# Graph tile periods: output biases and part of a table's weighing moved from VectorE to GpSimd

## The chip, the cores and the metric

The kernel runs on one core of a Trainium2 chip. The metric is the device time of one execution in microseconds. The core has TensorE (PE: matrix products), VectorE (DVE), ScalarE (ACT) and GpSimd (POOL) as computing engines, each with its own queue that is worked off in order; SyncE (SP) and GpSimd issue the transfers that are spoken of here. Times of the timeline count from the start of the profiled span.

## The reference

Two layers work on 625 nodes with 1024 features and 10,000 edges. What matters here is the first layer, which adds a graph attention and a linear attention to x, and then a small quantised feed-forward block:

```python
xn = _layernorm(x, axis=-1)
x = x + _L0_gnn_ref(xn, edge_index, ...) + _L0_mix_ref(xn[None], ...)[0]
x = x + _L0_ffn_ref(_layernorm(x, axis=-1)[None], ...)[0]
xn = _layernorm(x, axis=-1)
...
# in _L0_gnn_ref: softmax over the edges of a node, per head, then the weighted sum of rows
p = jnp.exp(e - m[dst])
denom = jax.ops.segment_sum(p, dst, num_segments=n)
alpha = p / (denom[dst] + 1e-16)
out = jax.ops.segment_sum(alpha[..., None] * xl[src], dst, num_segments=n)
out = out.reshape(n, HID)
return out @ W_up
# the end of _L0_mix_ref
return out @ W_o + b_o
```

`b_o` is the output bias, a row of 1024 that is added to every node.

## The kernel before, in words

The 625 nodes are cut into NT = 5 tiles of P = 125. The scores of all edges (4 heads) have been scattered into a table in HBM, indexed by source and destination. `CT` in SBUF holds how often each pair of nodes is an edge. The attention of tile t is then a dense product: the table's columns of tile t are weighed with `CT`, which gives `pT` (5 source tiles of 125 x 4 x 125), and `pT` is multiplied with the rows `xl1`.

The part of the code that is changed runs in periods p = 0 to 6, one tile entering per period. The functions, with their lines in the kernel before:

- `load_table(t)` (L851) loads the table's part for tile t into a tile `tb`, in two transfers issued by GpSimd.
- `weigh(t)` (L858) makes `pT`: five multiplications, one for each source tile s (L865), of `tb` (read with a step of four words, since the heads lie innermost) by `CT`, 125 x 500 each, all on VectorE. A second path of the program, `shifted`, is for other data and is not the one that runs here.
- `sums(t)` (L888) multiplies on TensorE: for each head, over s = 0 to 4 in this order, into the PSUM tile `pg`; then VectorE divides by the sums (`dens`, `den`, `go`, L898 to L902).
- `turn_sums(t)` transposes `go` (`pgoT`), and ScalarE copies it (`goT`). `up_again(t)` (L920) multiplies by `W_up` into `px`, which already holds the linear attention's output product, and VectorE adds `px` to x (L933).
- `add_bias(t, ...)` (L1070, L1074) adds the output bias to x, in two halves of 512 columns per tile. For t = 3 it adds `kept`, which holds the linear attention's output with its bias.
- `ffn(t)` (L964) is the feed-forward block of tile t, in steps `p1` (layer norm statistics, L950 to L975, and quantisation, L958 to L962, into `room`), `f1` (transposes, L985), `f2` (product `pgu` and gating), `f3` (transposes, `hT`, L1017), `f4` (product `pdn`, added to x, L1033), `p5` (layer norm for the next layer, L1040) and `f5` (transposes, L1048).
- `mixed(4, ...)` (L764) and `spacer()` (key and value products of the next layer, `pk` and `pv`, with `bk_t` and `bv_t` as biases) put other matrix products between these.

What is issued first runs first on each engine; TensorE's work is handed out through a small stream object, `do`, which issues each product one step before what follows it. Before the first period, GpSimd issues the loads of table 0, of x tile 0, of table 1, and of x tiles 1 to 4, each tile in two transfers; after them in its queue come the memset of `xnT1` (L1093), the load of `bq` (L238), and the loads of tables 2, 3 and 4 as buffers come free. The tiles `tb`, `pT`, `kept` and others share a pool of four buffers (`mid`).

Before the loop stand `load_table(0)`, the loads of x with `load_table(1)` between them, and `weigh(0)`. In period p come, in this order: the last steps of the feed-forward of tile p - 2, the first of tile p - 1, `sums(p)`, `turn_sums(p)`, `weigh(p + 1)`, `load_table(p + 2)`, the biases of this period, further feed-forward steps and `up_again(p)`. The biases of tiles 0 and 1 are added at the end of period 0, of tile 3 at the end of period 1, and of tiles 2 and 4 near the start of period 2.

Of the kernel before, what the change touches and what calls it, by code (L numbers as in the profile page):

```python
# [14 lines left out]
ALU = mybir.AluOpType  # L15
# [6 lines left out]
P = 125  # L22
# [20 lines left out]
def gps_kernel(tc: tile.TileContext, w: dict, out: bass.AP):  # L43

    again = attempt(tc, w, out, False)
    with tc.If(again > 0):
        attempt(tc, w, out, True)  # L50
# [3 lines left out]
def attempt(ctx: ExitStack, tc: tile.TileContext, w: dict, out: bass.AP, shifted: bool):  # L54

    nc = tc.nc
# [101 lines left out]
    def nodes(t):  # L158
        return slice(t * P, (t + 1) * P)
# [18 lines left out]
    def rows_dma(eng, dst, src):  # L178

        return [eng.dma_start(out=dst[lo:hi], in_=src[lo:hi]) for lo, hi in ((0, 112), (112, P))]  # L180
# [5 lines left out]
    CT = CTr if shifted else CTr.bitcast(FP)  # L186
# [38 lines left out]
    def mid(shape, name):  # L225
        return midp.tile(shape, FP, tag="mid", name=name)

    def bigT(name):
        return big.tile([128, KC, NP], FP, tag="big", name=name, padded_shape=[128, KC, 640])
# [133 lines left out]
    with ExitStack() as st0:  # L363
# [8 lines left out]
        with ExitStack() as edges:  # L372
# [385 lines left out]
            def mixed(t, ks=range(KC), keep=None, then=None, paced=True, cs=(0, 1)):  # L758
                for c in cs:
                    def pe(c=c):  # L760
                        if c == 0 and ks[0] == 0:
                            hold["px", t] = ps2("px1")
                        for k in ks:
                            made = nc.tensor.matmul(hold["px", t][:P, c, :], lhsT=oT[:, k, nodes(t)], rhs=wo[c](k),  # L764
                                                    start=(k == 0), stop=(k == KC - 1 and keep is not None))
                        latest["pe"] = made.ins.name

                    def after():
                        px = hold.pop(("px", t))
                        for c in range(2):  # L770
                            nc.vector.tensor_tensor(keep[:, c, :], px[:P, c, :], bo[c][:P], op=ALU.add)

                    do(None, pe, after if keep is not None and c == 1 else None)
                    if then is not None and c == 0:
                        then()
                    if paced:
                        work(0.87 * len(ks))
# [49 lines left out]
            bo = [lin.bias(w["L0_bo"], c, tag) for c, tag in enumerate(("bk_t", "bv_t"))]  # L827
# [4 lines left out]
            kept = mid([P, 2, 512], "kept")  # L832
# [14 lines left out]
        x = xpool.tile([P, NT, D], FP, name="x")  # L847
# [3 lines left out]
        def load_table(t):  # L851

            hold["tb", t] = mid([P, NT, P, 4], "tb")
            if not shifted:
                rows_dma(nc.gpsimd, hold["tb", t].rearrange("p s d h -> p s (d h)"),
                         tview[:, :, t * 4 * P:(t + 1) * 4 * P])

        def weigh(t):  # L858

            tb, pT = hold.pop(("tb", t)), mid([P, NT, 4, P], "pT")  # L860
            hold["pT", t] = pT
            if shifted:
                exps(t, tb)
            for s in range(NT):
                nc.vector.tensor_tensor(pT[:, s], tb[:, s].rearrange("p d h -> p h d"),  # L865
                                        CT[:, s, nodes(t)].unsqueeze(1).to_broadcast([P, 4, P]), op=ALU.mult)

        def exps(t, tb):

            for h in range(4):  # L870
                sc = mix.tile([P, NP], FP, tag="qe", name="sc", bufs=1)[:, 0:N].unsqueeze(2)
                nc.sync.dma_start(out=sc, in_=table[0:N * N, :].rearrange("(t p s) h -> t p s h", t=NT, p=P)
                                  [t][:, :, h:h + 1])
                mx = late.tile([P, 1], FP, tag="mx", name="mx", bufs=1)
                nc.vector.tensor_reduce(mx, sc, AX.XY, ALU.max)
                nc.vector.tensor_scalar(mx, mx, -1.0, None, op0=ALU.mult)
                nc.scalar.activation(sc, sc, AF.Exp, bias=mx, scale=1.0)
                for s in range(NT):
                    def pe():
                        pp = ps1("pexT")  # L880
                        nc.tensor.transpose(pp[:P, :P], sc[:, nodes(s), 0], ident[:P, :P])
                        nc.vector.tensor_copy(tb[:, s, :, h], pp[:P, :P])

                    do(None, pe)
# [3 lines left out]
        def sums(t):  # L888
            pT = hold.pop(("pT", t))

            def pe():
                pg4 = hold["pg"] = ps1("pg")[:, :260].rearrange("p (h e) -> p h e", h=4)
                for h in range(4):
                    group(pg4[:P, h, :], [(pT[:, s, h, :], xl1[:, s, h, :]) for s in range(NT)])

            def after():
                pg4 = hold["pg"]
                nc.vector.tensor_scalar(dens[:, t, :], pg4[:P, :, 64], 1e-16 if shifted else 1e-30, None, op0=ALU.add)  # L898
                den = late.tile([P, 4], FP, tag="den", name="den", bufs=2)
                nc.vector.reciprocal(den, dens[:, t, :])  # L900
                go = hold["go"] = late.tile([P, 4, 64], FP, tag="go", name="go", bufs=1)
                nc.vector.tensor_tensor(go, pg4[:P, :, 0:64],  # L902
                                        den.unsqueeze(2).to_broadcast([P, 4, 64]), op=ALU.mult)

            do(None, pe, after)
# [147 lines left out]
            return p1, f1, f2, f3, f4, p5, f5  # L1053


        load_table(0)
        for t in range(NT):
            rows_dma(nc.gpsimd, x[:, t, :], xrows[t])
            if t == 0:
                load_table(1)  # L1060
        weigh(0)
        kv_pieces = iter([(f, t) for t in range(NT) for f in ("key", "value")])
        made_of = {}

        def spacer():

            f, t = next(kv_pieces)
            getattr(lin1, f)(t)

        def add_bias(*ts):  # L1070
            for t in ts:
                for c in range(2):
                    xc = x[:, t, c * 512:(c + 1) * 512]
                    nc.vector.tensor_tensor(xc, xc, kept[:, c, :] if t == 3 else bo[c][:P], op=ALU.add)  # L1074

        for p in range(NT + 2):
            do()
            if p >= 2 and p != NT:
                made_of[p - 2][5]()
            if 1 <= p <= NT:  # L1080
                made_of[p - 1] = ffn(p - 1)
                made_of[p - 1][0]()
            if p == 1:
                mixed(4, cs=(0,))
            if p == 2:
                add_bias(2, 4)
            if p >= 3:
                spacer()
            if p >= 2 and p != NT:
                made_of[p - 2][6]()  # L1090
            if p == 0:
                xnT1 = bigT("xnT1")
                nc.gpsimd.memset(xnT1[:, :, N:NP], 0.0)  # L1093
                lin1 = LinearAttention(xnT1, ("L1_Wq", "L1_Wk", "L1_bk", "L1_Wv", "L1_bv"), w["L1_bq"],
                                       lambda us: None, nc.gpsimd)
                lin1.large = True
            if p < NT:
                sums(p)
            if 1 <= p <= NT:
                made_of[p - 1][1]()  # L1100
                do()
                if p == NT:
                    made_of[p - 2][5]()
                made_of[p - 1][2]()
                if p == NT:
                    made_of[p - 2][6]()
            do()
            if p < NT:
                turn_sums(p)
            if p + 1 < NT:  # L1110
                weigh(p + 1)
            if p + 2 < NT:
                load_table(p + 2)
            if p < 2:
                add_bias(*((0, 1), (3,))[p])
            if p == 1:
                mixed(4, cs=(1,))
                lin1.weights(0)
                lin1.half(0, loaded=True)
            if 2 <= p <= NT:  # L1120
                spacer()
            if 1 <= p <= NT:
                made_of[p - 1][3]()
            do()
            if p < NT:
                up_again(p)
            if 1 <= p <= NT:
                made_of[p - 1][4]()
# [625 lines left out]
    for i in range(3):  # L1754
        d = 1 << i
# [240 lines left out]
```

## Time and profile before

| What | Value |
|---|---|
| median of 3 runs (range) | 2218.25 us (2213.3 to 2223.8) |
| profiled execution: its time, its span | 2215.67 us, 2213.9 us |
| TensorE clock granted, mean over the span | 0.979 of full speed |
| stretch 425 to 437 us: PE busy, DVE busy, POOL busy, share of the DMA engines | 0.00, 0.52, 6.83 us, 0.61 |
| stretch 437 to 454 us: PE, DVE, POOL, DMA | 13.91, 9.86, 4.55 us, 1.02 |
| stretch 454 to 489 us: PE, DVE, POOL, DMA | 28.27, 23.37, 1.40 us, 0.53 |
| stretch 489 to 506 us: PE, DVE, POOL, DMA | 15.40, 10.50, 3.27 us, 0.27 |
| stretch 506 to 590 us: PE, DVE, POOL, DMA | 77.00, 59.43, 0.00 us, 0.10 |
| L865, a weighing of 125 x 500 on VectorE, 25 of them | 1040 ns each |
| L1074, a bias addition of 125 x 512 on VectorE, 10 of them | 682 ns each |
| L1249, an addition of 125 x 1024 on GpSimd (later stage), 10 of them | 2348 ns each (median) |

A line of the timeline gives the start, the time from start to end of a group of like instructions, the engine, the line of the kernel, the operation, what it writes and reads, and how many; the bracket gives the idle time of that engine just before, and what ended it. A line of the waits gives who waited for whom, then the sum in microseconds, how often, and the longest. Busy times of neighbouring instructions overlap slightly, so a row of five weighings takes 4.84 us and not 5 x 1.04.

### The profile page before, as it was taken

To read this page: it belongs to the slowest core of one execution; us is meant where nothing else is said; L and a number is where in the kernel's file an instruction comes from. 1 tells how busy PE (TensorE), PEld (TensorE's weight loads), DVE (VectorE), ACT (ScalarE), POOL (GpSimd) and SP (SyncE) were. 2 spreads that over 40 slices of the span, in tenths; PEclk is the share of its full clock that TensorE was granted. 3 is DMA by queue.
4 is the path that set the end of the run, shared out by engine and by line. 5 is a ranking of instruction groups with operands and counts; after the bars stand their busy time and mean duration, and the time that the engine had idled before them with its cause. 6 is when DMAs were issued, how large, how long until landed. Compare 5 with 4: busy or idle time off the path is not lost. (4 is left out here: it accounts for less than half of the span.)

```text
span 2213.9 us, 17370 instructions
## 1 busy us (share of the span) xinstructions
PE 2113.7 (95%) x6934; PEld 1211.5 (55%) x6934; DVE 713.6 (32%) x1214; ACT 193.9 (9%) x354; POOL 340.0 (15%) x349
## 2 busy tenths in 40 slices
PE   8999899489899999999999999999999999999998
PEld 6565475255455777754446767457744444444443
DVE  5776378367532660000123133322011111111012
ACT  2000110012211100000000111100000000000000
POOL 1666656500000100210000000110000000000011
PEclk9999999789999999999999999999999999999999
DMA  7532263351122110240213111022099988997742
GB/s 221 201 101 82 79 199 104 74 155 33 39 86 76 48 38 1 86 149 32 76 38 105 38 38 38 28 96 89 8 362 344 330 309 294 330 330 285 277 141 91
DMA packets 145848, 301.62 MB, mean 136 GB/s; under 512 B 12370, under 2 KB 22436, under 8 KB 145754
## 3 DMA queue, kind: packets, MB, share of 16 engines
q1 hardware_dynamic: 123700, 244.23, 31.1%
q0 software_dynamic: 17376, 46.42, 7.0%
q10 hardware_dynamic: 4678, 9.72, 1.4%
q8 instruction: 58, 0.95, 0.2%
q14 instruction: 36, 0.29, 0.0%
HBM read 277.49 MB, written 22.84 MB: 136 GB/s over the span
## 5 line engine op out<-in xcount | busy, mean ns | idle before, releaser
L137 PE MATMUL pu<-w,xgT 128*128 128x512 f32 x768 | 333.9, 593 | 1.9 <-DVE xgT L1290 1.9
L137 PEld LDWEIGHTS pu<-w,xgT 128*128 128x128 f32 x768 | 144.0, 190 | 174.8 <-issue 172.0
L137 PE MATMUL pyb<-w,hb 128*128 128x512 f32 x384 | 174.3, 598 | 2.5 <-ACT yb L105 2.1
L137 PE MATMUL pq<-xnT,w 128*128 128x313 f32 x512 | 141.0, 435 | 7.0 <-DVE v L293 7.0
L137 PE MATMUL pv<-w,xnT 128*125 128x512 f32 x320 | 143.9, 600 | 3.7 <-issue 3.1
L137 PE MATMUL pk<-w,xnT 128*125 128x512 f32 x320 | 142.9, 598 | 1.8 <-issue 1.4
L137 PE MATMUL p<-tT,w 128*128 128x313 f32 x512 | 136.3, 428 | 0.4 <-DVE tT L1290 0.4
L137 PEld LDWEIGHTS pq<-xnT,w 128*128 128x128 f32 x512 | 98.9, 194 | 47.3 <-DVE v L293 7.8
L137 PEld LDWEIGHTS pyb<-w,hb 128*128 128x128 f32 x384 | 69.8, 189 | 90.9 <-issue 74.8
L1830 DVE TENSOR_TENSOR su<-pu,su 128x512 f32<-128x512 f32 x24 | 16.6, 691 | 314.6 <-ACT su L1829 314.6
L137 PEld LDWEIGHTS p<-tT,w 128*128 128x128 f32 x512 | 96.8, 190 | 37.9 <-issue 1.2
L137 PEld LDWEIGHTS pv<-w,xnT 128*125 128x125 f32 x320 | 60.2, 190 | 79.1 <-issue 77.4
L137 PEld LDWEIGHTS pk<-w,xnT 128*125 128x125 f32 x320 | 59.8, 189 | 73.9 <-issue 73.2
L641 POOL DMA_INDIRECT table<-es,at x79 | 84.6, 1071 | 61.2 <-issue 30.6
L1813 POOL DMA_INDIRECT xg<-rows_d,slots x12 | 11.3, 943 | 524.8 <-PE pxg L1820 449.0
L621 POOL DMA_INDIRECT ga<-xl_d,si x79 | 79.3, 1004 | 46.8 <-issue 21.6
L621 POOL DMA_INDIRECT gb<-xr_d,di x79 | 80.6, 1021 | 25.8 <-issue 25.8
L764 PE MATMUL px<-w,oT 128*125 128x512 f32 x160 | 69.8, 594 | 2.1 <-DVE x L933 1.4
L1179 DVE TENSOR_TENSOR z<-pz,z 125x512 fp32r<-125x512 f32 x10 | 6.9, 692 | 196.8 <-ACT z L1177 196.8
L137 PE MATMUL px<-w,hT 128*125 128x512 f32 x160 | 70.3, 592 | 0.0
L137 PE MATMUL px<-w,oT 128*125 128x512 f32 x160 | 70.3, 592 | 0.0
L137 PE MATMUL ph<-meanT,w 128*128 128x313 f32 x256 | 70.1, 426 | 0.0
(363 smaller groups left out, 2521.5 us busy)
## 6 DMA issues: line engine op xcount, KB each, us to landing
w<-in_eW_dram SPq DMA_DIRECT2D x144, 1024.0 KB
w<-in_L_Wk_dram SPq DMA_DIRECT2D x8, 1024.0 KB
w<-in_L_Wv_dram SPq DMA_DIRECT2D x8, 1024.0 KB
w<-in_L_Wq_dram SPq DMA_DIRECT2D x8, 1024.0 KB
w<-in_L_Wo_dram SPq DMA_DIRECT2D x8, 1024.0 KB
w<-in_W_self_dram SPq DMA_DIRECT2D x8, 1024.0 KB
w<-in_W_neigh_dram SPq DMA_DIRECT2D x8, 1024.0 KB
w<-in_sW_dram SPq DMA_DIRECT2D x8, 1024.0 KB
```

The source lines that it names most:

```text
L137: made = nc.tensor.matmul(dst, lhsT=lhsT, rhs=rhs, start=(i == 0), stop=(i == len(pairs) - 1))
L621: got = nc.gpsimd.indirect_dma_start(out=ab[g][side][0:p, j, :], out_offset=None, in_=src[:, :], in_offset=bass.IndirectOffsetOnAxis(ap=ix ...
L641: nc.gpsimd.indirect_dma_start(out=table[:, :], out_offset=bass.IndirectOffsetOnAxis(ap=at[0:p, lo + j:lo + j + 1], axis=0), in_=es[0:p, l ...
L764: made = nc.tensor.matmul(hold["px", t][:P, c, :], lhsT=oT[:, k, nodes(t)], rhs=wo[c](k), start=(k == 0), stop=(k == KC - 1 and keep is no ...
L1179: nc.vector.tensor_tensor(low, src, high.bitcast(FP), op=ALU.subtract)
L1813: nc.gpsimd.indirect_dma_start(out=xg, out_offset=None, in_=rows_d[:, :], in_offset=bass.IndirectOffsetOnAxis(ap=slots[:, b:b + 1], axis=0))
L1830: nc.vector.tensor_tensor(su, pu[:, 0, :], su, op=ALU.mult)
```

## The change

Three edits in the periods of the first layer:

1. `weigh`: of the five source tiles, s = 0 to 2 stay on VectorE and s = 3 and 4 are issued on GpSimd, in each of the five periods.
2. `add_bias` issues on GpSimd and no longer on VectorE.
3. Its calls move: tiles 0 and 1 before the loop, after the loads of x and ahead of `weigh(0)`; tiles 2, 4 and 3 together at the end of period 0, after `weigh(1)` and `load_table(2)`.

```diff
             for s in range(NT):
-                nc.vector.tensor_tensor(pT[:, s], tb[:, s].rearrange("p d h -> p h d"),
-                                        CT[:, s, nodes(t)].unsqueeze(1).to_broadcast([P, 4, P]), op=ALU.mult)
+                eng = nc.vector if shifted or s < 3 else nc.gpsimd
+                eng.tensor_tensor(pT[:, s], tb[:, s].rearrange("p d h -> p h d"),
+                                  CT[:, s, nodes(t)].unsqueeze(1).to_broadcast([P, 4, P]), op=ALU.mult)
...
+        def add_bias(*ts):
+            for t in ts:
+                for c in range(2):
+                    xc = x[:, t, c * 512:(c + 1) * 512]
+                    nc.gpsimd.tensor_tensor(xc, xc, kept[:, c, :] if t == 3 else bo[c][:P], op=ALU.add)
+
         load_table(0)
         for t in range(NT):
             rows_dma(nc.gpsimd, x[:, t, :], xrows[t])
             if t == 0:
                 load_table(1)
+        add_bias(0, 1)
         weigh(0)
...
-        def add_bias(*ts):
-            for t in ts:
-                for c in range(2):
-                    xc = x[:, t, c * 512:(c + 1) * 512]
-                    nc.vector.tensor_tensor(xc, xc, kept[:, c, :] if t == 3 else bo[c][:P], op=ALU.add)
...
-            if p == 2:
-                add_bias(2, 4)
...
-            if p < 2:
-                add_bias(*((0, 1), (3,))[p])
+            if p == 0:
+                add_bias(2, 4, 3)
```

GpSimd's queue thus reads, after the last load of x: four additions (tiles 0 and 1), the two weighings of table 0, the memset, the load of `bq`, the two weighings of table 1, the load of table 2, six additions (tiles 2, 4 and 3), the two weighings of table 2, the load of table 3, the loads of `bk_t` and `bv_t` for the next layer, a memset, the weighings of table 3, the load of table 4 and the weighings of table 4. The products on TensorE keep their order.

## The prediction

> **What bounds the kernel now.** I read the page first, for the limiting engine, then the waits of the stretch that the change touches (425 to 625 us), then the timeline of that stretch engine by engine, because a change in one stage is worth what the wait that ends last there is worth.
>
> ```profile
> PE 2113.7 (95%) x6934; PEld 1211.5 (55%) x6934; DVE 713.6 (32%) x1214; ACT 193.9 (9%) x354; POOL 340.0 (15%) x349
> ```
>
> TensorE is busy 95% of the span and VectorE 32%, so work taken off VectorE pays only where TensorE stands still for VectorE. The waits of this stretch say where that is:
>
> ```profile
> PE pg L137 <- DVE pT L865: 32.2, 5, 31.1
> POOL x L180 <- DMA tb<-table: 7.0, 4, 3.7
> PE px L764 <- DVE x L933: 1.4, 1, 1.4
> ```
>
> One wait counts: 31.1 us in one piece before the first product `pg`, until VectorE has weighed the first table (L865). It is really a wait for the table's DMA; VectorE starts within the microsecond after it lands. The second line shows GpSimd held up several times between its own loads of x. The timelines of TensorE, then VectorE, then GpSimd:
>
> ```profile
> 441.37 6.98 PE L137 MATMUL pg<-xl,pT 125*125 125x65 f32 x32 [0.27 <-DVE pT L865]
> ...
> 450.49 5.67 PE L928 MATMUL px<-wu,goT 128*125 128x512 f32 x8 [0.53 <-ACT goT L916]
> 457.60 7.13 PE L764 MATMUL px<-w,oT 128*125 128x512 f32 x16 [1.43 <-DVE x L933]
> ```
>
> ```profile
> 436.48 4.84 DVE L865 TENSOR_TENSOR pT<-tb,CT 125x500 f32<-125x500 f32 x5 [16.19 <-DMA tb<-table]
> ...
> 449.14 4.86 DVE L865 TENSOR_TENSOR pT<-tb,CT 125x500 f32<-125x500 f32 x5
> 453.92 0.67 DVE L1074 TENSOR_TENSOR x<-x,bk_t 125x512 f32<-125x512 f32 x1
> ...
> 456.33 1.21 DVE L933 TENSOR_TENSOR x<-px,x 125x1024 f32<-125x1024 f32 x1
> ```
>
> ```profile
> 444.02 0.52 POOL L180 DMA_DIRECT2D x<-in_x_dram  x1 [0.50 <-DMA tb<-table]
> ...
> 445.57 0.60 POOL L238 DMA_DIRECT2D bq<-in_L_bq_dram  x1 [0.91 <-DMA x<-in_x_dram]
> ```
>
> See three things. The first weighing ends at 436.48 + 4.84 = 441.32, and TensorE runs its next 32 matmuls from 441.37: a path without slack. GpSimd, in contrast, is issuing loads of x until 444.02 + 0.52 = 444.54. And in the next step VectorE is hardly late: `px` (L928) ends at 450.49 + 5.67 = 456.16, and the addition that needs it (L933) starts at 456.33.
>
> [...] L1249, 1024 columns, takes 2348 ns. [...] in the other stage where GpSimd adds:
>
> ```profile
> 771.87 1.58 DVE L340 SCALAR_TENSOR_TENSOR qf<-qe,qf 128x626 f32<-128x626 f32 x1 [2.15 <-ACT qf L339]
> 773.37 2.57 DVE L1198 TENSOR_SCALAR xh<-x,mv,rs 125x512 f32<-125x512 f32 x1
> ...
> 776.63 2.28 DVE L1179 TENSOR_TENSOR xnl<-xh,xnh 125x512 fp32r<-125x512 f32 x1 [0.69 <-ACT xnh L1177]
> ```
>
> These three take 0.81, 0.54 and about 0.69 us elsewhere, and here stretch to the end of the GpSimd addition that runs beside them (one runs from 776.02 to 778.37). [...] PEclk is 0.50 from 437 to 454 and 0.51 from 489 to 506.
>
> **The change, part by part.**
>
> *First weighing, the part that decides.* VectorE keeps s = 0 to 2, GpSimd gets s = 3 and 4. But GpSimd works in order, and in its queue the two instructions stand behind all loads of x and behind the new `add_bias(0, 1)`. So: loads end at 444.54, as before (their waits are for table and x transfers, which the change leaves alone). Then four additions of 125x512. [...] half of the 2.32 us spacing in the trace, 1.16 us, is its floor. I take 1.25: 5.0 us, until 449.5. x of period 1 must have landed for the third of them; the load of `bq`, which waited for that, went at 445.57, so this doesn't hold it. Then two weighings of 500 columns: 1.25 us each if the 16-byte step of the table costs GpSimd nothing. On VectorE the same shape takes 1.04 us against 0.68 for a plain 512[...]. Bounds 1.15 and 1.8, taken 1.6: 3.2 us, until 452.7. [...] TensorE goes on at 452.8 instead of 441.37: +11.4 us. Nothing covers it: the 32 matmuls left, then `go`, `pgoT` and `px`, all follow in a chain. The bounds give 3.2 + 4.7 + 2.3 = 10.2 and 3.2 + 5.2 + 3.6 = 12.0.
>
> *Biases off VectorE in the first step.* Four additions (453.92 to 456.33, 2.4 us) and two weighings leave VectorE ahead of L933, but L933 then waits for `px`: gain 456.33 - 456.16 = 0.17 us. GpSimd runs its six further additions beside the three weighings left. [...] VectorE needs 3 x 1.0 + 2 x 1.25 = 5.5 us after its start at 449.14, until 454.7, still before 456.16 (all in times of before; everything here moves by the same 11 us). Cost 0.
>
> *Biases off VectorE later.* The pair for t = 3 (481.47 to 482.67) stood before `hT` (L1017), with `px` on TensorE until 483.27; the four for t = 2 and 4 (495.20 to 497.7) stood before a wait of 3.35 us for `pg`. Gain 0.
>
> *Weighing of periods 2 to 4.* GpSimd's part waits for the table's transfer, the earlier buffer and, ahead of it in the queue, bias loads and a memset that waits for `pg`; by my reading of the waits it runs in the gaps near 460, 480 and 531, well before VectorE's part at 476.6, 508.9 and 537.8. At 460 it blocks L975 and L962 by up to 3 us, and `room` (done at 462.97) is wanted only at 468.88. In the period at 537 the weighing is late for TensorE:
>
> ```profile
> 537.75 4.92 DVE L865 TENSOR_TENSOR pT<-tb,CT 125x500 f32<-125x500 f32 x5
> ...
> 545.56 1.21 DVE L933 TENSOR_TENSOR x<-px,x 125x1024 f32<-125x1024 f32 x1
> ```
>
> `px` ends at 545.26 and L933 starts at 545.56: gain at most 0.3 us. Elsewhere L933 starts with the end of `px`. The table loads that follow in GpSimd's queue (tb 3 and tb 4) are wanted 20 us later at the earliest: 0.
>
> Sum: +11.4 - 0.2 - 0.3 = +10.9 us, on the profiled execution 2215.67 (span 2213.9 and 1.8 around it), so 2226.6. The median of the runs shown is 2218.25, 2.6 above that execution; the result will be such a median, so I forecast 2218.25 + 10.9 = 2229 us, which is +0.48%.
>
> **The rivals.**
>
> *More than the queue.* [...] the second weighing of VectorE waits for all six additions, until about 450.1 + 6 x 1.25 = 457.6, and does its two others after, until 459.6: L933 is 3.3 us late, and the sum is +14 us, 2232. For it: the full blocking above. Against it: there VectorE got in at the next boundary between two GpSimd additions.
>
> *Not slower: the clock pays it back.* The half clock from 489 to 506 costs 7 us: `pg` takes 8.66 us there against 4.58 in the next period, `pgu` 3.28 against 1.97, the transposes about 2 more. It follows an idle stretch of only 4.05 us (485.6 to 489.65). [...] 10.9 - 7 = +4 us, 2222, within 0.5%; it decides once the half-clock stretch is gone. For it: the runs shown spread over 10.5 us, which something must make. Against it: the gap is made by VectorE's chain after `pdn`, which the change leaves alone.
>
> *Faster: VectorE's time is what counts.* Ten additions at 0.6 and ten weighings at 0.97 are 15.7 us of VectorE's time; if they all were on the path, 2218 - 15.7 = 2203. Against it: the waits, in which TensorE waits for L865 only once.
>
> **How the numbers follow.** 0.5%, about what a measurement of this kernel can tell from no change, is 11.1 us, and so my forecast stands just at the bound. The forecast's case gets 0.60, of which I count 0.38 above the bound: the step's cost may be the greater, and the chance in the two medians falls both ways. More than the queue 0.20; the clock 0.12; faster 0.08. So slower 0.38 + 0.20 = 0.58, same 0.22 + 0.12 = 0.34, faster 0.08. The range of the likeliest alone, with its bounds and the spread of a median, is 2226 to 2232; to hold 8 in 10 it reaches to the second and third case: 2220 to 2236.
>
> **What would show it.** In the changed kernel's timeline: the fourth and fifth stretch of `pg` released by GpSimd, the 32 matmuls starting at 452 to 453 us; four GpSimd additions of 1.2 to 1.3 us from 444.5 and two weighings of 1.2 to 1.8 after them; L934 (now) starting with the end of `px`. I am wrong if the first weighing on GpSimd ends before 447, if later periods are each shorter than before by over 1 us, or if the half-clock stretches differ between the two traces.

## The result, and the profile after

The change makes the kernel slower: median 2233.19 us (2226.66 to 2238.23, 10 runs) against 2217.43 us (2211.8 to 2223.8, 10 runs) before; the ratio is 1.0063, with a 95% interval of 1.0045 to 1.0080. That is 15.8 us between the medians, where the forecast had 10.9. The ratio is formed from the single runs and not from the two medians (their quotient is 1.0071); by it the loss is some 14 us. The same holds for the ratios below.

The profiled execution has a span of 2231.3 us, 17.4 more than before. The page's busy times hardly move where it matters; they show only that work went from VectorE to GpSimd:

```profile
PE 2113.2 (95%) x6934; PEld 1212.2 (54%) x6934; DVE 706.3 (32%) x1194; ACT 194.1 (9%) x354; POOL 367.7 (16%) x369
```

TensorE's busy time is the one of before (2113.7) within half a microsecond, so on balance the added time is idle time of TensorE. The waits of the changed stretch, 425 to 642 us, say where (sum, times, longest):

```profile
PE pg L137 <- POOL pT L866: 11.4, 1, 11.4
...
PE px L764 <- DVE x L934: 4.3, 1, 4.3
```

The first is new: TensorE waits for GpSimd's part of the first weighing. The second was 1.4 us. GpSimd's timeline in the changed kernel:

```profile
449.58 0.52 POOL L180 DMA_DIRECT2D x<-in_x_dram  x1 [0.53 <-DMA tb<-table]
450.12 1.27 POOL L1061 TENSOR_TENSOR x<-x,bk_t 125x512 f32<-125x512 f32 x1
...
455.01 2.93 POOL L866 TENSOR_TENSOR pT<-tb,CT 125x500 f32<-125x500 f32 x2
...
466.76 1.27 POOL L1061 TENSOR_TENSOR x<-x,bk_t 125x512 f32<-125x512 f32 x1
...
471.66 2.47 POOL L1061 TENSOR_TENSOR x<-x,kept 125x512 f32<-125x512 f32 x2
```

The last load of x is issued until 450.10, four additions stand between it and the two weighings, and these end at 457.94 (the bracket of the 32 matmuls below names the short memset that follows them in GpSimd's queue). Six more additions run from 466.76 to 474.13 without a break. TensorE's and VectorE's timelines beside that:

```profile
457.99 6.98 PE L137 MATMUL pg<-xl,pT 125*125 125x65 f32 x32 [0.76 <-POOL xnT L1093]
...
467.11 5.73 PE L929 MATMUL px<-wu,goT 128*125 128x512 f32 x8 [0.53 <-ACT goT L917]
477.09 8.83 PE L764 MATMUL px<-w,oT 128*125 128x512 f32 x16 [4.25 <-DVE x L934]
```

```profile
441.44 2.94 DVE L866 TENSOR_TENSOR pT<-tb,CT 125x500 f32<-125x500 f32 x3 [16.55 <-DMA tb<-table]
...
465.76 1.03 DVE L866 TENSOR_TENSOR pT<-tb,CT 125x500 f32<-125x500 f32 x1
...
466.71 8.24 DVE L866 TENSOR_TENSOR pT<-tb,CT 125x500 f32<-125x500 f32 x1
...
474.88 1.02 DVE L866 TENSOR_TENSOR pT<-tb,CT 125x500 f32<-125x500 f32 x1
475.83 1.21 DVE L934 TENSOR_TENSOR x<-px,x 125x1024 f32<-125x1024 f32 x1
```

Three readings. First, the 32 matmuls start 457.99 - 441.44 = 16.55 us after VectorE's first weighing starts; before it was 441.37 - 436.48 = 4.89. So the first delay is 11.7 us. Second, one instruction of the second weighing, which takes 1.0 us elsewhere, lasts 8.24: it covers the whole run of six additions, and it ends only after the last of them. The addition after `px` (L934) therefore starts at 475.83, 3.0 us after `px` ended (467.11 + 5.73 = 472.84). Third, TensorE then stands for 4.25 us, and its next product (L764) runs for 8.83 us instead of 7.13 at a lower clock: the granted clock (PEclk) is 0.63 from 477 to 481 us, and in the profile of before it is 1.00 over this product. The blocked instruction counts as busy in this profile (8.24 us): only the length of a single one shows that it waited.

The first weighing itself starts 4.96 us later than in the profile of before (441.44 against 436.48). Nothing that the change touches stands ahead of it, and in the three profiles of the changed kernel it starts at 441.4, 444.7 and 453.8 us (the last two on one chip), so I don't count it to the change and measure everything below from this start.

The profile of before also lost time in a place that this one did not. The second `pg` starts 485.75 - 464.56 = 21.2 us later than in the profile of before, but at the end of the span only 17.4 us of this are left. Of the difference 3.0 us lie in the next layer's products, where the profile of before has a product at the lower clock (first line, PEclk 0.77 over its length) and this one has not (second line, PEclk 1.00):

```profile
603.86 9.14 PE L137 MATMUL pv<-w,xnT 128*125 128x512 f32 x16
```

```profile
623.42 7.03 PE L137 MATMUL pv<-w,xnT 128*125 128x512 f32 x16
```

The two other profiles of the changed kernel have 7.03 and 9.12 us at this place, so I don't count this to the change either.

### The profile page after: what moved, and what is told of

Same layout as the page of the kernel before. It is cut to its first block, busy times and chain, and to the rows that moved or that the text cites. A ratio compares the mean times of both kernels' runs of the same rounds, so it can differ in the third digit from the quotient of the medians.

```text
span 2231.3 us, 17368 instructions
## 1 busy us (share of the span) xinstructions
PE 2113.2 (95%) x6934; PEld 1212.2 (54%) x6934; DVE 706.3 (32%) x1194; ACT 194.1 (9%) x354; POOL 367.7 (16%) x369
## 5 line engine op out<-in xcount | busy, mean ns | idle before, releaser
L1830 DVE TENSOR_TENSOR su<-pu,su 128x512 f32<-128x512 f32 x24 | 16.6, 691 | 314.6 <-ACT su L1829 314.6
L1813 POOL DMA_INDIRECT xg<-rows_d,slots x12 | 11.4, 950 | 524.7 <-PE pxg L1820 448.9
L764 PE MATMUL px<-w,oT 128*125 128x512 f32 x160 | 71.5, 606 | 6.3 <-DVE x L934 4.3
L137 PE MATMUL pg<-xl,pT 125*125 125x65 f32 x200 | 32.0, 332 | 45.5 <-DVE pT L866 32.0
```

Of the source, the lines that this page charges most:

```text
L137: made = nc.tensor.matmul(dst, lhsT=lhsT, rhs=rhs, start=(i == 0), stop=(i == len(pairs) - 1))
L1813: nc.gpsimd.indirect_dma_start(out=xg, out_offset=None, in_=rows_d[:, :], in_offset=bass.IndirectOffsetOnAxis(ap=slots[:, b:b + 1], axis=0))
L1830: nc.vector.tensor_tensor(su, pu[:, 0, :], su, op=ALU.mult)
```

## The experiments

Two theories, one for each delay. Queue theory: GpSimd's part of the first weighing stands behind its loads of x and four additions. Port theory, as the expectations call it: six additions in a row on GpSimd keep VectorE's second weighing out. The runs can show which instructions hold up which; that a port which both need does it was my assumption, and no run shows it. The rivals: that the first delay comes from the loads and not from who weighs; that the second comes from splitting the weighing, or from chance. The runs were made on several chips, so each is compared with the kernel before on its own chip.

**First weighing on VectorE.**

```diff
-                eng = nc.vector if shifted or s < 3 else nc.gpsimd
+                eng = nc.vector if shifted or s < 3 or t == 0 else nc.gpsimd
```

> The changed kernel, with all five parts of the first table's weighing on VectorE again. Counted from the start of that weighing, the 32 matmuls of the first pg start 4.89 us later in the kernel before and 16.55 us later in the changed one; the product mixed(4) (L764) starts 21.1 and 35.7 us later. Queue theory (GpSimd's part stands behind the loads of x and four additions): the 32 matmuls start at +4.9 again, and 11.7 us come back. Port theory (GpSimd's run of additions keeps VectorE's second weighing out): this loss isn't undone by the edit; GpSimd now still adds and weighs around the second weighing, so mixed(4) starts between +21 and +27 us. Time 0 to 5 us above the kernel before, 2217 to 2222. Rival (the delay comes from the loads, not from who weighs): the 32 matmuls stay near +16.

Measured: 2201.95 us against 2193.02, ratio 1.0049 (1.0032 to 1.0066). The 32 matmuls start at +4.89 us, as in the kernel before. But VectorE's second weighing takes longer still (its timeline, then TensorE's):

```profile
427.48 5.34 DVE L866 TENSOR_TENSOR pT<-tb,CT 125x500 f32<-125x500 f32 x1
...
432.75 7.14 DVE L866 TENSOR_TENSOR pT<-tb,CT 125x500 f32<-125x500 f32 x1
...
439.81 1.98 DVE L866 TENSOR_TENSOR pT<-tb,CT 125x500 f32<-125x500 f32 x1
```

```profile
442.98 9.97 PE L764 MATMUL px<-w,oT 128*125 128x512 f32 x16 [9.06 <-DVE x L934]
```

GpSimd's timeline beside that:

```profile
426.71 1.26 POOL L1061 TENSOR_TENSOR x<-x,bv_t 125x512 f32<-125x512 f32 x1
427.92 0.10 POOL L1093 MEMSET xnT<- 128x8 f32 x1
...
428.57 2.94 POOL L866 TENSOR_TENSOR pT<-tb,CT 125x500 f32<-125x500 f32 x2
...
432.94 1.28 POOL L1061 TENSOR_TENSOR x<-x,bk_t 125x512 f32<-125x512 f32 x1
```

The first part is held until GpSimd's own two weighings are over (431.51) and ends 1.3 us after them, the second is held for five of the six additions. One thing here fits no simple rule: the first part stands from 427.48, and between 427.97 and 428.57 GpSimd runs only a small memset and issues a transfer, yet the part doesn't get in. mixed(4) starts at +28.2 us, a microsecond beyond the expected window, and the time is above it as well (8.9 us for 0 to 5). So the queue theory holds for the first delay, and one delay was partly hidden by the other: with the queue's delay gone, VectorE comes to its second weighing while GpSimd still has two weighings and six additions to do. The port theory holds in kind (VectorE is held up beside GpSimd's weighings and additions), and its size was too small.

**Biases back on VectorE.** The kernel before, with edit 1 alone.

> The kernel before, with only the weighing changed (parts 3 and 4 of every table on GpSimd, biases on VectorE in their old places). Queue theory: GpSimd begins its part of the first weighing when its loads of x are issued, 8.1 us after VectorE's start, and needs 2.9 us, so the 32 matmuls start at +11.1 us. Port theory: no run of additions on GpSimd, so TensorE's idle time ahead of mixed(4) is about 1.4 us as before, and mixed(4) takes 7.1 us. Together +6.2 us on the kernel before, some 2223 to 2224. If the second loss has to do with the split weighing itself, the idle time ahead of mixed(4) stays near 4.3 us.

Measured: 2200.44 us against 2193.02, ratio 1.0039 (1.0025 to 1.0054), 7.4 us for 6.2 expected. TensorE's timeline, in which VectorE's first weighing starts at 416.00:

```profile
427.28 6.98 PE L137 MATMUL pg<-xl,pT 125*125 125x65 f32 x32 [0.76 <-POOL xnT L1094]
...
436.39 6.51 PE L929 MATMUL px<-wu,goT 128*125 128x512 f32 x8 [0.53 <-ACT goT L917]
444.23 7.13 PE L764 MATMUL px<-w,oT 128*125 128x512 f32 x16 [1.32 <-DVE x L934]
```

The 32 matmuls start at +11.28, and the second delay is gone: 1.32 us of idle time, and 7.13 us for mixed(4), as before. The rest of the 7.4 us is `px`, which takes 6.51 us instead of 5.67. The split of the weighing is thus not what makes the second delay; on its own it costs the time for which GpSimd's loads of x and its two weighings outlast VectorE's weighing.

**Only the later biases back on VectorE.**

```diff
+            if p == 2:
+                add_bias(2, 4)
...
-            if p == 0:
-                add_bias(2, 4, 3)
+            if p == 1:
+                add_bias(3)
```

Here `add_bias` takes the engine as an argument: GpSimd for tiles 0 and 1, VectorE for the others.

> The changed kernel, with the biases of tiles 2, 4 and 3 on VectorE again in their old places; those of tiles 0 and 1 stay on GpSimd ahead of the first weighing. Queue theory: the 32 matmuls stay at +16.5 us. Port theory: VectorE's second weighing takes 3 us instead of 10.1, TensorE's idle time ahead of mixed(4) falls from 4.25 to about 1.4 us, mixed(4) from 8.8 to 7.1 us, and 4.6 us come back: 2227 to 2229. If the port isn't the cause, the second weighing still takes 10 us.

Measured: 2204.70 us against 2193.02, ratio 1.0058 (1.0041 to 1.0075). The expected times of these first runs were given on the scale of another chip; here it meant, as a difference to the kernel before (2217), 10 to 12 us, and 11.7 was measured. VectorE's timeline, then TensorE's:

```profile
441.79 2.95 DVE L866 TENSOR_TENSOR pT<-tb,CT 125x500 f32<-125x500 f32 x3
```

```profile
449.78 7.13 PE L764 MATMUL px<-w,oT 128*125 128x512 f32 x16 [1.32 <-DVE x L934]
```

The 32 matmuls start at +15.7 us, the second weighing takes 2.95 us, TensorE idles 1.32 us and mixed(4) takes 7.13. The six additions are the cause of the second delay, which is gone with them.

**All weighing on VectorE.** The changed kernel without edit 1.

> The changed kernel, with all weighing on VectorE; all biases stay on GpSimd in their new places. Queue theory: the 32 matmuls start at +4.9 us. Port theory: the six additions stand beside the second weighing, now five instructions; VectorE gets one or two of them in before GpSimd's run of about 7.4 us, the rest after it, so the addition after px comes about 5 us late, TensorE idles 6 us ahead of mixed(4), and the half clock adds 1 to 2 us: 5 to 7 us above the kernel before, 2222 to 2225. Without the port's blocking the time is that of the kernel before.

Measured: 2194.24 us against 2193.02, ratio 1.0010 (1.0003 to 1.0017): 1.2 us for 5 to 7 expected. TensorE idled 3.5 us ahead of mixed(4), for 6 expected. The two engines did meet, but took turns. VectorE's timeline, then GpSimd's, of this kernel:

```profile
429.12 1.98 DVE L866 TENSOR_TENSOR pT<-tb,CT 125x500 f32<-125x500 f32 x1
...
431.03 1.98 DVE L866 TENSOR_TENSOR pT<-tb,CT 125x500 f32<-125x500 f32 x1
...
432.93 2.00 DVE L866 TENSOR_TENSOR pT<-tb,CT 125x500 f32<-125x500 f32 x1
```

```profile
430.41 1.76 POOL L1061 TENSOR_TENSOR x<-x,bk_t 125x512 f32<-125x512 f32 x1
432.14 1.95 POOL L1061 TENSOR_TENSOR x<-x,bv_t 125x512 f32<-125x512 f32 x1
434.06 1.94 POOL L1061 TENSOR_TENSOR x<-x,bk_t 125x512 f32<-125x512 f32 x1
```

Each addition and each weighing is now stretched to about 1.95 us: one of each in 1.92 us. No run of additions passes VectorE. My expectation that VectorE would wait for GpSimd's whole run failed here.

So edit 1 alone costs 7.4 us and the moved biases alone 1.2, but both together 15.8: the rest comes from their meeting, once in GpSimd's queue ahead of the first weighing and once beside the second.

**GpSimd weighs ahead of the first biases.**

```diff
-        add_bias(0, 1)
         weigh(0)
+        add_bias(0, 1)
```

> The changed kernel, with GpSimd's part of the first weighing issued ahead of the biases of tiles 0 and 1 instead of behind them. Queue theory: only the loads of x are still ahead, so the 32 matmuls start 11.1 to 11.3 us after VectorE's first weighing starts (16.55 in the changed kernel, 15.7 in the run with late biases on VectorE): about 5 us come back, and +6.3 remain. Port theory: the six later additions still meet the second weighing, so VectorE's three parts take 8 us or more and TensorE idles 4 us or more ahead of mixed(4). Together 9 to 12 us above the kernel before.

The 32 matmuls start at +11.27 us: the four additions are 4.6 to 5.3 us of the first delay, taking 15.9 (two later profiles, below) and 16.55 for the changed kernel. In the profile VectorE took turns again, so the port theory's part of the expectation failed: the second weighing took 6.1 us, and TensorE idled 1.37 us. The time is 2233.79 us against 2219.65, ratio 1.0044 (1.0021 to 1.0067). Its nine times fall into two groups, 2220 to 2226 and 2234 to 2236, so the median says little; the ratio stands for 9.8 us, with 9 to 12 expected. Do the groups differ in whether VectorE is kept out? A second profile:

> The kernel with GpSimd's part of the first weighing ahead of the biases, a second look. Its nine times fell in two groups, 2220 to 2226 and 2234 to 2236 us, and its profile, of the lower group, showed VectorE and GpSimd taking turns. [...] this look shows either turns again (second weighing 6.1 us, TensorE idle 1.4 us ahead of mixed(4)) or VectorE kept out of the run of additions (10 us or more, idle 4 us or more, a time some 10 us higher). If the groups come from something else, turns again whatever the time.

Measured: 2218.12 us (2217.44 before), turns once more, 6.10 us and 1.37 us, with the 32 matmuls at +11.65. Neither profile fell into the upper group, so what makes it stays open.

**A memset between the additions.** After each bias addition GpSimd sets a spare tile.

```diff
+        spare = late.tile([P, 512], FP, name="spare")
...
                     nc.gpsimd.tensor_tensor(xc, xc, kept[:, c, :] if t == 3 else bo[c][:P], op=ALU.add)
+                    nc.gpsimd.memset(spare, 0.0)
```

> The changed kernel, with a memset of a spare 125x512 tile on GpSimd after every bias addition, an instruction that reads no SBUF. Queue theory: four memsets of some 0.5 us stand ahead of the first weighing too, so the 32 matmuls start at 18 to 18.7 us. Port theory, if VectorE is kept out because GpSimd's next reading instruction is ready when one ends: [...] VectorE's second weighing takes 4 to 6 us and TensorE idles 1.4 us ahead of mixed(4). [...]

Measured: 2231.24 us against 2219.65, ratio 1.0056 (1.0038 to 1.0074). The 32 matmuls start at +17.84 us, just short of the 18 to 18.7 expected. GpSimd's and VectorE's timelines at the second weighing:

```profile
464.02 1.28 POOL L1063 TENSOR_TENSOR x<-x,bk_t 125x512 f32<-125x512 f32 x1
465.23 0.54 POOL L1064 MEMSET spare<- 125x512 f32 x1
465.71 1.52 POOL L1063 TENSOR_TENSOR x<-x,bv_t 125x512 f32<-125x512 f32 x1
```

```profile
463.97 2.17 DVE L866 TENSOR_TENSOR pT<-tb,CT 125x500 f32<-125x500 f32 x1
...
466.07 1.99 DVE L866 TENSOR_TENSOR pT<-tb,CT 125x500 f32<-125x500 f32 x1
```

As in the changed kernel, VectorE's second instruction stands ready as the first addition begins (463.97 and 464.02, there 466.71 and 466.76). There it waited for all six; here it ends at 466.14, 0.84 us after the first addition (465.30), so it ran beside the memset. The three parts take 5.05 us, TensorE idles 1.32 us and mixed(4) takes 7.13. In this program a memset after each addition was enough to let VectorE in. That the memset itself does it is not shown beyond this one profile: two other programs take turns without one, and the 0.10 us memset ahead of GpSimd's weighing in the first experiment let nothing in.

**The changed kernel again, and two others.** Is it chance whether VectorE is kept out?

> The changed kernel itself, a second look. In its profile VectorE's second weighing (three parts) took 10.1 us, kept out by six additions in a row; in the runs with all weighing on VectorE, and with the first weighing ahead of the biases, VectorE and GpSimd took turns on like instructions. If being kept out belongs to the program (which instruction stands ready when), the three parts take about 10 us again and TensorE idles about 4.3 us ahead of mixed(4). If it is chance in each execution, they may as well take 5 to 6 us, with an idle time of 1.4 us.

> The changed kernel itself, a third look: as for the second. 10 us if it belongs to the program; by chance, either.

> The kernel with all of the first weighing on VectorE and the rest as changed, a second look. In its first profile the second weighing took 14.3 us, with TensorE idle for 9.1 us ahead of mixed(4). If it belongs to the program: 14 us and 9 us again. If it is chance: 5 to 14 us.

> The kernel with all weighing on VectorE and the biases on GpSimd, a second look. In its first profile the two engines took turns (1.9 us for one of each) and the second weighing's five parts took 9.4 us. If it belongs to the program: 9.4 us and turns again. If it is chance: up to 13 us, with a run of additions that VectorE is kept out of.

Measured: the second weighing took 10.12 and 10.12 us in the changed kernel (10.14 at first), 14.47 with the first weighing on VectorE (14.31), and 9.66 with all weighing there (9.43, turns both times). VectorE's timelines of the two profiles of the changed kernel:

```profile
468.40 10.12 DVE L866 TENSOR_TENSOR pT<-tb,CT 125x500 f32<-125x500 f32 x3
```

```profile
477.44 10.12 DVE L866 TENSOR_TENSOR pT<-tb,CT 125x500 f32<-125x500 f32 x3
```

TensorE's idle time ahead of mixed(4) was 3.6 and 3.3 us for 4.3 expected, since `px` ahead of it took longer (6.36 and 6.62 us, 5.73 at first). So being kept out belongs to the program. Not chance, then; but what in the program decides between turns and being kept out I can't say: in both kinds VectorE's instruction was already waiting when an addition ended. The single times were 2236.81, 2249.25, 2218.18 and 2217.42 us (2213.97 before), too few to compare; the second one's first weighing started at 453.78 us, some 9 us later than the first one's (444.71).

**A version to beat both.** The kernel before, with the first load of x held until table 0 has landed, so that no load of x or of table 1 runs beside the table's.

```diff
-                rows_dma(nc.gpsimd, hold["tb", t].rearrange("p s d h -> p s (d h)"),
+                hold["loads"] = rows_dma(nc.gpsimd, hold["tb", t].rearrange("p s d h -> p s (d h)"),
...
-            rows_dma(nc.gpsimd, x[:, t, :], xrows[t])
+            got = rows_dma(nc.gpsimd, x[:, t, :], xrows[t])
             if t == 0:
+                if not shifted:
+                    for table0 in hold["loads"]:
+                        behind(got[0], table0.ins.name)
```

> A version meant to beat both: the kernel before, with the first load of x, and so all that follow in GpSimd's queue, held until table 0 has landed. In the kernel before the load of table 0 is issued 8.2 us ahead of VectorE's start while loads of x and table 1 share the DMA engines. If sharing is what makes it long, table 0 lands 1.5 to 2.5 us sooner, and the time falls by as much, about 2191 (ratio 0.999). If the load is as long alone, nothing changes at the start, and tables and x come up to 6 us later; table 1 is wanted 12.7 us after the start, so the cost is 0 to 3 us.

Measured: 2217.14 us against 2219.65, ratio 0.9994 (0.9978 to 1.0011): no difference that can be told. The profile says why:

```profile
429.93 1.55 POOL L180 DMA_DIRECT2D tb<-table  x2 [1.66 <-issue]
438.39 1.10 POOL L180 DMA_DIRECT2D x<-in_x_dram  x2 [6.91 <-DMA tb<-table]
```

VectorE starts at 437.79, 7.86 us after the issue, against 8.24 before: the table's load is almost as long with those loads held back, and between these two profiles that was worth 0.4 us. The long idle time ahead of the first `pg` isn't shortened this way.

The runs that change the weighing or the biases, counted from the start of VectorE's first weighing, in microseconds (the last column is the difference of the medians):

| Kernel | 32 matmuls start | idle ahead of mixed(4) | mixed(4) takes | second pg starts | time against before |
|---|---|---|---|---|---|
| before | 4.9 | 1.4 | 7.1 | 28.1 | |
| changed, three profiles | 16.6, 15.9, 15.9 | 4.3, 3.6, 3.3 | 8.8, 9.9, 10.2 | 44.3, 44.8, 45.0 | +15.8 |
| first weighing on VectorE, two profiles | 4.9, 4.9 | 9.1, 8.7 | 10.0, 8.8 | 38.0, 36.9 | +8.9 |
| biases on VectorE | 11.3 | 1.3 | 7.1 | 35.2 | +7.4 |
| later biases on VectorE | 15.7 | 1.3 | 7.1 | 38.4 | +11.7 |
| all weighing on VectorE, two profiles | 4.9, 4.9 | 3.5, 4.4 | 7.1, 8.8 | 30.2, 32.2 | +1.2 |
| GpSimd's first weighing ahead, two profiles | 11.3, 11.7 | 1.4, 1.4 | 7.1, 7.1 | 34.0, 34.6 | +14.1 (two groups; 9.8 by the ratio) |
| memset between | 17.8 | 1.3 | 7.1 | 41.3 | +11.6 |

The start of the second `pg` in the first profile of each row, against 28.1 before, gives the measured time within 2 us in every row but the one with two groups.

## Why the prediction was right or wrong

It was right in the direction and in the cause of the larger part; the change was put 4.9 us too small, because the smaller part was put at nothing. The result, 2233.19, lies within the range, next to the first rival's 2232, and that rival's case, not the likeliest one, is what the traces show.

- *First weighing.* Predicted +11.4 us; measured 16.55 - 4.89 = 11.7 in the first profile and 11.0 in the two later ones. Its terms, which were my estimates, held: the additions took 1.25 to 1.27 us (taken 1.25), the weighings 2.93 for two (taken 3.2), and the matmuls had no slack: they started 0.05 us after the weighings ended. The loads of x, taken to end 8.1 us after VectorE's start, ended after 8.0 us in the later profiles but after 8.7 in the first; that the first one agrees so closely with 11.4 is partly luck, since this makes up for the shorter weighings. Putting the first weighing back took the whole delay away; putting only the order of biases and weighing right took about 5 us of it.
- *Second weighing, the step that failed.* I had GpSimd and VectorE take turns, three weighings of 1.0 us and two additions of 1.25 in 5.5 us, and wrote "Cost 0". Measured: 10.1 us in each of three profiles, VectorE kept out until all six additions were done. (Where another program did take turns around a weighing of three parts, they took 6.1 us.) The first rival had this case with 3.3 us for the late addition after `px`; measured 2.8 us more idle time than before (4.25 against 1.43). What neither had is the clock: the longer stop is followed by 8.8 to 10.2 us for mixed(4) instead of 7.1, another 1.7 to 3.1 (PEclk 0.63 from 477 to 481 us in the first profile). So 10.9 + 2.8 + 1.7 is 15.4, about the 15.8 measured. I chose turns because of a single case, L340 in the stage at 772 us, which got in at a boundary (it ran from 771.87 to 773.45, and the next GpSimd addition began at 772.74); one case didn't carry that. What decides between turns and being kept out stays open, and so does what the two engines contend for.
- *Gains.* Small, as predicted: in the period of the fourth weighing, from the start of `pk` to that of `pv`, 12.0 us instead of 12.25. The first step's 0.17 us can't appear, since L934 was late.
- *The clock that pays it back.* Refuted for the stretch that it named: the third `pg`, after the stop that it spoke of, takes 8.66 us in every run, as before, and the stop, 4.05 us, and the clock after it, PEclk 0.50 in both profiles, are the same too. The sign that I gave for being wrong, lower-clock stretches that differ between the two traces, did appear in the stretch from 590 us on (9.14 against 7.03 us for one product, above), but the changed kernel shows both lengths there.
- *Faster, by VectorE's time.* Refuted: VectorE has 20 instructions less, and the kernel is slower.

## What to carry to other kernels

Before work moves to another engine, read what stands ahead of it in that engine's queue at that place: here the moved weighing itself took 2.9 us, and the queue ahead of it made the delay 11. In these traces GpSimd's additions and weighings held up VectorE's weighings, 1.98 us for one of 1.0 where they took turns and 8.24 where VectorE was kept out; put such work where VectorE is idle, or where what it delays isn't awaited. And a stall of TensorE like the ones here should be priced with what comes after it as well as with its length: in six of seven profiles with a stop of 3.3 to 9.1 us ahead of mixed(4), this product took 1.6 to 3.1 us longer.

## What the runs showed that I had not expected

- Between GpSimd's additions and VectorE's weighings, one program takes turns (1.92 us for one of each, 1.95 us per instruction) and another keeps VectorE out for a whole run (8.24 us for an instruction of 1.0), each the same way in every profile. With a memset after each addition VectorE got in; a gap of 0.6 us without any addition or weighing on GpSimd, in the two profiles with the first weighing on VectorE, did not let it in.
- Undoing the larger delay made the smaller one grow: with the first weighing back on VectorE, TensorE's stop ahead of mixed(4) went from 4.25 to 9.06 us.
- After a stop of 3.3 to 3.6 us ahead of mixed(4) the product took 9.9 and 10.2 us in two profiles, and 7.13 us in another (3.5 us of idle time). The stop's length alone doesn't decide it; after 1.3 to 1.4 us, in seven profiles, the product always took 7.13.
